# Inputs of grouped quads laid by rounds, source rows asked for six items ahead, prepared data written an item later

## The chip, the cores and the metric

The kernel runs on one core of one Trainium2 chip. Times are device microseconds of one execution; lower is better. The time before is 2416.06 us, the median of three runs (2413.56 to 2433.85).

## The reference

A graph layer with 6,250 nodes, 200,000 edges sorted by target, 128 features and 20 edge attributes:

```python
h = relu(layernorm(x))
xw = h @ W_in
W_ij = (softplus(edge_attr @ W_f1 + b_f1) - log 2) @ W_f2 + b_f2
W_ij = W_ij * edge_weight
out = segment_sum(xw[dst] * W_ij, src, 6250)
return x + (softplus(out @ W_o1 + b_o1) - log 2) @ W_o2 + b_o2
```

The target of an edge (`dst`, sorted) says which row of `xw` is read, and the source (`src`, random) says into which row the product is summed.

## The kernel before

Edges are handled in quads of 512 (four chunks of 128), 391 in all. `Plan` orders them into 414 **items**: 207 single quads ("S"), 184 grouped quads ("B") in 23 **rounds** of eight, and 23 items "V" for what overflows from a round. After the first dozen items S and B take turns, so a round spans 17 items.

The order of work is written out by hand. The main loop (line 1304) runs once per item i, and at named points of it calls hooks that were registered with `at(i, point, function, ...)`: "L" at the beginning (loads), "D0" to "D2" and "DM" (VectorE), "A0" to "A2" (ScalarE), "PE2" (TensorE), "S" at the very end. Each engine takes its instructions in that order, and SyncE (SP), which issues nearly all loads and writes, does so too: an issue that has to wait for its data holds everything behind it.

An item's own work: `s1_pe` makes the first layer's matmul, one item ahead; `s1_exp` (line 362, one instruction an item) and `s1_ln` make the softplus; `s2_pe_w` the second layer; `s2_m` (line 604) multiplies by the gathered rows. A single quad is then compared for equal sources and scattered to DRAM by POOL with indirect DMAs that add (`scatter`, line 672). The single quads 16 to 191 are "listed": in windows of 16 their comparisons are made ahead by `l_eq` (line 418), two quads at a time, at point "DM", where `s2_m` of the item stands behind it.

What the change touches:

- **Source rows.** `sb_load` (line 385) brings the 512 sources of each of two quads, spread to all partitions, 128 KB a row, into a tile `sb` with four buffers. `s1_eq` (line 403) and `l_eq` read it. For the listed quads it is asked for two items ahead of `l_eq` (line 1257), for the others two items ahead of the quad. The first window's rows are needed at items 6 to 13, interleaved with the rows of the first single quads.
- **Inputs of a round.** `nat_load` (line 681) runs three items ahead of a round's ranking. The inputs lie in DRAM in the order of the edges, and a round takes every second quad. It issues four loads: the attributes `fn` (8 runs of 336 bytes a partition), the targets `dn` (8 runs of 16 bytes) and two for the window bases `bn` (each 8 runs of 8 bytes, the same for all partitions). `nat_1` to `nat_4` split `fn` in three bf16 parts into `sts`, `nat_max` (line 698) takes its largest value, and `nat_win` turns targets and bases into one-hot columns.
- **Preparation of nodes.** 25 groups of 256 nodes (the last of 128) go through layernorm and `W_in`; for all but the first the steps are spread over items t0-3 to t0+3, one group about every nine items, the last at items 213 to 216. `prep_x3` (line 266) makes the last part, and `tab_write` (line 271), called from it at point "D2" of item t0+3, writes the group to the DRAM table `tab`, from which `load_pair` and `load_win` read windows. `base_caps` (line 1661) keeps a window's start within the groups that are written by then.
- **Features of single quads.** `fb_1` to `fb_4` split 4,096 edges at a time; `fb_4` ends with the write to `fsd` (line 297), from which `load_pair` takes `ft`. `load_pair` runs `SLEAD` = 4 items ahead of its first quad and has three buffers.

Further lines that the profile names: 188 `xt_load`, 277 `fb_load`, 313 to 321 `load_pair`, 328 `load_win`, 687 to 690 `nat_load`, 500 `l_load`, 653 `s3_ji`.

Of the kernel before, what the change touches and what calls it, by code (L numbers as in the profile page):

```python
# [7 lines left out]
F32 = mybir.dt.float32  # L8
BF16 = mybir.dt.bfloat16
I32 = mybir.dt.int32  # L10
# [4 lines left out]
AX = mybir.AxisListType  # L15
# [5 lines left out]
P = 128  # L21
# [19 lines left out]
PLEAD = 7  # L41
WLEAD = 6
SLEAD = 4
CQ = 16
EARLY_N = 256
BLK = 4
# [6 lines left out]


@with_exitstack
def tile_gnn(ctx: ExitStack, tc: tile.TileContext, x, fS, fN, cT, srcT, srcr, dstr, dstT, base0, win_, wf1, wfB, wf2,
             bias, bo1c, wo1, wo2, consts, sel, ident, cmap, out, n_edges):
    nc = tc.nc
    N = out.shape[0]
# [202 lines left out]
    def prep_x3(g):  # L262
        o, T = groups[g]
        w = T * P
        x3 = pst[g]["x3"]
        nc.vector.tensor_tensor(x3[:, :T, 2], pst[g]["rm"][:, :T], x3[:, :T, 1], op=ALU.subtract)
        tab_write(g)

    def tab_write(g):
        o, T = groups[g]  # L270
# [23 lines left out]
    def fb_4(b):  # L294
        f3 = fst[b]["f3"]
        nc.vector.tensor_tensor(f3[:, 2], fst[b]["fr"], f3[:, 1], op=ALU.subtract)
        nc.sync.dma_start(fsd[b].rearrange("g (p e) -> p g e", p=P), f3)
        del fst[b]

# [374 lines left out]

    rk = {}

    def cols(t, w, q, d, n):
        v = t[:, w * q:w * (q + d * (n - 1)) + w]
        return v if n == 1 else bass.AP(v.tensor, v.offset, [v.ap[0], [w * d, n], [1, w]])

    def nat_load(r):
        fn = wk.tile([P, RND, 4 * KN], F32, tag="fn", name="fn", bufs=1)
        dn = wk.tile([P, RND, 4], I32, tag="dn", name="dn", bufs=1)
        bn_ = wk.tile([P, 2, RND, 2], I32, tag="bn0", name="bn0", bufs=1)
        for j, dj, q, d, n in runs(pl.rounds[r]):
            v = slice(j, j + dj * (n - 1) + 1, dj)
            nc.sync.dma_start(fn[:, v] if n > 1 else fn[:, j], cols(fN, 4 * KN, q, d, n))
            nc.sync.dma_start(dn[:, v] if n > 1 else dn[:, j], cols(dstT, 4, q, d, n))
            for k in range(2):
                nc.sync.dma_start(bn_[:, k, v] if n > 1 else bn_[:, k, j],  # L690
                                  cols(base0[k:k + 1].to_broadcast([P, base0.shape[1]]), 2, q, d, n))
        rk[r] = {"fn": fn.rearrange("p j (c k) -> p (j c) k", k=KN), "dn": dn, "bn": bn_}

    def nat_1(r):
        nc.scalar.copy(sts[r % 2][:, :, 1:1 + KN], rk[r]["fn"])

    def nat_max(r):
        nc.vector.tensor_reduce(fmax[:, NB + r:NB + r + 1], rk[r]["fn"].rearrange("p x k -> p (x k)"), axis=AX.X,
                                op=ALU.max, apply_absolute_value=True)

    def nat_2(r):
# [11 lines left out]
    def nat_win(r):  # L713
        t = sts[r % 2]
        b = wk.tile([P, RND, 2], F32, tag="nb", name="nb", bufs=1)
        nc.vector.scalar_tensor_tensor(b, rk[r]["bn"][:, 0], 0.0, rk[r]["bn"][:, 1], op0=ALU.max, op1=ALU.min)
        rel = wk.tile([P, RND, 2, 2], F32, tag="nrel", name="nrel", bufs=1)
        nc.vector.tensor_tensor(rel.rearrange("p j h c -> p (j h) c"), rk[r]["dn"].rearrange("p j (h c) -> p (j h) c", c=2),
                                b.rearrange("p j h -> p (j h)").unsqueeze(2).to_broadcast([P, 2 * RND, 2]), op=ALU.subtract)
        for h in range(2):  # L720
            o = t.rearrange("p (j h c) k -> p h j c k", h=2, c=2)[:, h, :, :, KZ + h * WIN:KZ + (h + 1) * WIN]
            nc.vector.tensor_tensor(o, rel[:, :, h].unsqueeze(3).to_broadcast([P, RND, 2, WIN]),
                                    iot[:, :WIN].unsqueeze(1).unsqueeze(1).to_broadcast([P, RND, 2, WIN]), op=ALU.is_equal)
# [220 lines left out]
    with tc.manual_schedule():  # L944
# [83 lines left out]
        prep_mm(0)  # L1028
        fb_3(0)
        fb_4(0)  # L1030
        rel0 = [rel(0, k * SEG, (k + 1) * SEG) for k in range(2)]
        prep_x1(0)
        prep_rm(0)
        prep_x2(0)
        prep_x3(0)
        for k in range(2):
            src_cast(0, k * SEG, (k + 1) * SEG, nc.gpsimd)
        ws = cp.tile([K1, P], BF16, name="ws")
# [29 lines left out]
        def at(i, point, fn, *a):  # L1068
            hooks.setdefault((i, point), []).append((fn, a))
# [31 lines left out]
        for g in range(1, NG):  # L1101
            t0 = pl.prep(g)
            at(t0 - 3, "L", xt_load, g)
            at(t0 - 1, "D2", prep_stat, g)
            at(t0, "A1", prep_rs0, g)
            at(t0, "D2", prep_norm, g)
            at(t0 + 1, "PE2", prep_tp, g)
            at(t0 + 2, "A0", prep_relu, g)
            at(t0 + 2, "PE2", prep_mm, g)
            at(t0 + 3, "A0", prep_x1, g)  # L1110
            at(t0 + 3, "DM", prep_rm, g)
            at(t0 + 3, "A2", prep_x2, g)
            at(t0 + 3, "D2", prep_x3, g)
        for b in range(1, NB):
            t0 = max(2, pl.ps[b * BE // SEG] - SLEAD - 4)
            if b > 1:
                at(max(0, t0 - 3), "L", fb_load, b)
            at(t0, "A1", fb_1, b)
            at(t0, "D2", fb_2, b)
            at(t0 + 1, "A1", fb_3, b)  # L1120
            at(t0 + 1, "D2", fb_4, b)

        busy = units | {pl.prep(g) + k for g in range(1, NG) for k in range(5)}
        mid = clear(NQ // 2, busy, 2) - 6
# [126 lines left out]
        for w in range(NW):  # L1251
            for g in range(4):
                n = LB + SW * (w - 1) + 4 * g
                i = pl.ps[n] + 2 if w else 6 + 2 * g
                for k in range(2):
                    kk = (LB + SW * w + 4 * g) // 2 + k
                    at(max(0, i + k - 2), "L", sb_load, kk)
                    at(i + k, "DM", l_eq, kk)
                if w:
                    i = clear(i + 2, units)  # L1260
                    at(i, "PE2", l_count, (LB + SW * w) // 4 + g)
                else:
                    at(i + 1, "PE2", l_count, LB // 4 + g, (0,))
                    i += 2
                    at(i, "PE2", l_count, LB // 4 + g, (1,))
                at(i + 1, "D0", l_dup, w, g)
            i += 1
            at(i, "D0", l_scan, w)
            i = clear(i, units)
            at(i, "PE2", l_before, w)  # L1270
            at(i + 1, "D0", l_index, w)
            assert i + 1 <= pl.ps[LB + SW * w] + 1
            at(i + 2, "D2", l_id, w)
            i = clear(i + 3, units)
            at(i, "PE2", l_place, w)
            at(i + 1, "D0", l_take, w)
            i = clear(wend[w] + 12, units)
            at(i, "L", l_start, w)
            at(i, "A0", l_dg, w)
            at(i, "PE2", l_row, w)  # L1280
            at(i + 1, "D0", l_same, w)
            k = clear(i + 1, units)
            at(k - 1, "L", l_load, w)
            at(k, "PE2", l_sum, w)
            at(k + 1, "A0", l_copy, w)
            at(k + 1, "DM", l_ji, w)
            at(k + 1, "A2", l_int, w)
            at(k + 2, "S", l_scatter, w)
# [86 lines left out]
    with tc.For_i(0, trips, 1) as ci:  # L1375
# [15 lines left out]
        sb = wk.tile([P, P], I32, bufs=1, tag="oeq", name="fsb")  # L1391
        nc.sync.dma_start(sb, srcr.rearrange("s e -> (s e)")[bass.ds(ci * P, P)].unsqueeze(0).to_broadcast([P, P]))
        fn = wk.tile([P, KN], F32, tag="fn", name="ffn", bufs=1)
        nc.sync.dma_start(fn, fN[:, bass.ds(ci * KN, KN)])
        fr = wk.tile([P, KN], F32, tag="nr", name="ffr", bufs=1)
        fp = wk.tile([P, KZ], BF16, tag="oh", name="ffp")
        nc.vector.memset(fp[:, 0:1], 1.0)
# [237 lines left out]
    return i  # L1635


def runs(qs):
    for step in (1, 2, 3):
        if all(qs[k + 2 * step] - qs[k + step] == qs[k + step] - qs[k] for k in range(len(qs) - 2 * step)):  # L1640
            return [(j, step, qs[j], qs[j + step] - qs[j], len(qs[j::step])) for j in range(step)]
    return [(j, 1, q, 1, 1) for j, q in enumerate(qs)]


def node_groups(n):
    first = min(EARLY_N, n)
    return [(0, first // P)] + [(o, min(2, (n - o) // P)) for o in range(first, n, 256)]
# [2 lines left out]
def base_caps(n, nq):  # L1650
    pl = Plan(nq)
    groups = node_groups(n)
    at = {}
    for k, q in enumerate(pl.sq):
        at[q] = pl.ps[k // 2 * 2] - SLEAD
    for q in pl.bo:
        at[q] = pl.perm[q] - WLEAD + 4
    caps = []
    for s in range(-(-nq // 2)):
        i = min(at[q] for q in (2 * s, 2 * s + 1) if q in at)  # L1660
        ready = min([groups[g][0] for g in range(1, len(groups)) if pl.prep(g) + 3 >= i] or [n])
        caps.append(ready - WIN)
    return caps


def _layout(inputs):
# [25 lines left out]
    caps[:-(-nq // 2)] = base_caps(np_, nq)  # L1692
    sq = np.array(pl.sq + [nq - 1] * (-len(pl.sq) % (be // SEG)))
    fs = fp.reshape(-1, SEG, rb)[sq].reshape(-1, be, rb).transpose(0, 2, 1)
    fn = np.concatenate([fp, cpad[:, None]], 1).reshape(-1, P, rb + 1).transpose(1, 0, 2).reshape(P, -1)
    base0 = np.stack([dstp[::WSEG], np.repeat(caps, SC // WSEG).astype(dstp.dtype)])
    sel = np.zeros((P, 3), np.float32)
    sel[[rb + 1, 2 * rb + 2, 3 * rb + 3], 0] = 1.0
    sel[KX, 1:] = 1.0
# [17 lines left out]
    for r in range(3):  # L1717
# [8 lines left out]
        "srcT": srcp.reshape(-1, P)[cols].T,  # L1726
        "srcr": srcp.reshape(-1, SC),
        "dstr": dstp.reshape(-1, SC),
        "dstT": dstp.reshape(-1, P).T,
        "base0": base0,  # L1730
        "win": np.asarray(inputs[p + "W_in"]),
        "wf1": np.concatenate([wf1] * 6 + [bf1[None]] * 3, 0),
# [30 lines left out]
```

## Time and profile before

| | |
|---|---|
| median of three runs | 2416.06 us |
| profiled execution | 2406.39 us, span 2404.6 us |
| mean granted TensorE clock | 0.863 |
| PE busy | 1975.6 us (82%) |
| PE weight loads | 1389.7 us (58%) |
| DVE busy | 1717.5 us (71%) |
| ACT busy | 1257.1 us (52%) |
| POOL busy | 1583.2 us (66%) |
| DMA packets | 419,278, 224.64 MB, 162,227 of them under 512 B |
| SP's wait at line 271 for the DVE | 376.1 us in 23 waits |
| SP's wait at line 297 for the DVE | 194.7 us in 16 waits |

Busy times of different engines lie beside each other. "A <- B" names an engine's instruction that stood idle and what ended that wait. A row of the windows view gives a stretch of the span in us, its length, the busy time of PE, PEld, DVE, ACT and POOL with the count of instructions, then the granted clock, the mean share of DMA time and GB/s. Instructions of the SP queue (SPq) take time to issue; the transfer itself runs afterwards.

### The profile page before, as it was taken

Reading aid. Unit: us, or ns where it says so; the run is one execution under the profiler, and the core shown is the slowest. Engines: PE = TensorE matmul, PEld = TensorE weight load, DVE = VectorE, ACT = ScalarE, POOL = GpSimd, SP = SyncE. Lnnn points to the kernel's source line nnn. Section 1 sums busy time; section 2 is a strip of 40 time slices with the busy share of each in tenths; the row PEclk is TensorE's granted clock in tenths of the full one; section 3 lists DMA queues with packets and bytes.
Section 4 is the critical chain, followed back from the end, with each engine's and each line's share of the span. In section 5 each row is a group of like instructions: output and inputs, shape, how many; then the busy total and the mean of one; then the engine's idle time right before and its main releaser. Section 6 shows DMA issues by size and latency. Waiting matters only on the chain. (4 is left out here: it accounts for less than half of the span.)

```text
span 2404.6 us, 58531 instructions
## 1 busy us (share of the span) xinstructions
PE 1975.6 (82%) x21648; PEld 1389.7 (58%) x21648; DVE 1717.5 (71%) x4480; ACT 1257.1 (52%) x3311; POOL 1583.2 (66%) x988
## 2 busy tenths in 40 slices
PE   2679878698897897997867988988988898999846
PEld 1567555465665565655645556656655665666734
DVE  4557669678777778867766778777878868776635
ACT  1357455455554565554545556555655555565424
POOL 4478757566666666674655676677677767776774
PEclk9678788788898888987978889988998988999867
DMA  6676544444554545544454454455455445445748
GB/s 204 181 168 112 89 73 76 83 74 82 91 74 75 91 79 90 83 69 78 70 88 71 83 90 74 73 92 86 71 87 92 76 76 79 73 68 87 148 47 233
DMA packets 419278, 224.64 MB, mean 93 GB/s; under 512 B 162227, under 2 KB 398550, under 8 KB 418990
## 3 DMA queue, kind: packets, MB, share of 16 engines
q0 software_dynamic: 135520, 67.56, 27.8%
q1 hardware_dynamic: 283038, 153.25, 24.1%
q8 instruction: 170, 2.79, 0.5%
q14 instruction: 118, 0.97, 0.1%
q10 hardware_dynamic: 432, 0.08, 0.0%
HBM read 121.80 MB, written 98.94 MB: 92 GB/s over the span
## 5 line engine op out<-in xcount | busy, mean ns | idle before, releaser
L672 POOL DMA_INDIRECT acc<-s,lji x704 | 1166.5, 1657 | 498.7 <-DVE s L604 174.0
L362 ACT ACTIVATE a<-z 128x512 f32<-128x512 f32 x414 | 252.2, 609 | 560.5 <-PE z L336 502.7
L577 PE MATMUL W<-w,a 128*128 128x128 f32 x3312 | 544.1, 314 | 0.0
L672 POOL DMA_INDIRECT acc<-s,ji x215 | 350.0, 1628 | 258.2 <-ACT ji L653 160.0
L577 PEld LDWEIGHTS W<-w,a 128*128 128x128 f32 x3312 | 457.6, 214 | 71.9 <-issue 53.6
L882 PE MATMUL un<-so,bm 32*128 32x392 bf16 x2944 | 342.8, 359 | 12.4 <-DVE ldup L434 5.6
L882 PE MATMUL un<-so,rem 32*128 32x392 bf16 x2944 | 330.1, 357 | 0.0
L882 PE MATMUL un<-so,low 32*128 32x392 bf16 x2944 | 326.1, 352 | 0.0
L604 DVE TENSOR_TENSOR s<-W,xc 128x512 f32<-128x512 f32 x230 | 158.7, 690 | 216.5 <-ACT xc L586 180.6
L367 ACT ACTIVATE a<-a,con 128x512 f32<-128x512 f32 x414 | 298.8, 722 | 13.6
L586 ACT ACTIVATE xc<-xg,cb 128x128 f32<-128x128 f32 x828 | 239.5, 386 | 95.3 <-PE xg L565 44.2
L797 DVE TENSOR_SCALAR pm<-iot,pos 128x576 bf16<-128x576 f16 x736 | 239.3, 387 | 26.1 <-PE po L809 25.2
L893 DVE TENSOR_TENSOR accT<-un,accT 128x392 f32<-128x392 f32 x352 | 174.2, 556 | 116.8 <-PE un L882 116.5
L808 PE MATMUL pf<-pm,st 128*108 128x512 bf16 x736 | 244.2, 423 | 6.4 <-ACT s L627 3.9
L594 ACT ACTIVATE xc<-xgb,ex 128x128 f32<-128x128 f32 x736 | 207.3, 363 | 0.0
L869 DVE TENSOR_SCALAR so<-iot,ex 128x392 bf16<-128x392 f16 x736 | 193.7, 325 | 0.0
L339 PE MATMUL xgb<-wb,bfe 42*128 42x128 bf16 x2208 | 190.5, 221 | 3.5 <-DVE accT L893 3.5
L418 DVE TENSOR_TENSOR eql<-sb,srcT_sb 128x1024 bf16<-128x1024 int16 x88 | 107.0, 1216 | 110.0 <-DMA sb<-src 100.9
L809 PE MATMUL po<-pm,st 128*108 128x64 bf16 x736 | 146.0, 198 | 41.4 <-DVE ex L832 33.6
L336 PE MATMUL z<-bfe,wsb 64*128 64x512 bf16 x552 | 178.4, 392 | 0.2
L565 PE MATMUL xg<-wn,oh 63*128 63x128 bf16 x828 | 92.4, 240 | 100.9 <-DVE oh L378 84.8
L882 PEld LDWEIGHTS <-bm 32*128 32x128 bf16 x2944 | 122.8, 101 | 90.4 <-issue 56.8
(233 smaller groups left out, 3239.1 us busy)
## 6 DMA issues: line engine op xcount, KB each, us to landing
sb<-src SPq DMA_DIRECT2D x207, 128.0 KB
rb<-reld SPq DMA_DIRECT2D x207, 64.0 KB
fsd<-f SPq DMA_DIRECT2D x26, 480.0 KB
ft<-fsd SPq DMA_DIRECT2D x103, 120.0 KB
acc<-s,lji POOLq DMA_INDIRECT x704
ta_in<-acc SPq DMA_DIRECT2D x36, 256.0 KB
fb<-in_fS_dram SPq DMA_DIRECT2D x26, 320.0 KB
ft<-fsd SPq DMA_DIRECT2D x103, 80.0 KB
```

Source lines behind the costliest of these rows:

```text
L336: yield nc.tensor.matmul(z, wsb[:n, k], ft[:n], start=(k == 0), stop=(k == 2))
L339: nc.tensor.matmul(xg[:, c, :], ft[KZ:KX, c * P:(c + 1) * P], wn[KZ:KX, k, :], start=(k == 0), stop=(k == 2))
L362: nc.scalar.activation(a, st[q]["z"], AF.Exp)
L367: nc.scalar.activation(a, a, AF.Ln, bias=half, scale=0.5)
L577: nc.tensor.matmul(W[:, c, :], st[n]["a"][:, c * P:(c + 1) * P], w2, start=False, stop=(c == 3))
L586: nc.scalar.mul(xc[:, c, :], st[n]["xg"][:, c, :], v)
L594: nc.scalar.mul(xc[:, c, :], xg[:, c, :], bq[q]["ex"][:, c, 0:1])
L672: nc.gpsimd.indirect_dma_start(out=accs[k][:rows, :], out_offset=bass.IndirectOffsetOnAxis(ap=ji, axis=0), in_=s, in_offset=None, compute_ ...
L797: nc.vector.tensor_scalar(pm[:, c], iot[:, :SLOTS], rk[r]["pos"][:, 4 * j + c:4 * j + c + 1], None, op0=ALU.is_equal)
L808: nc.tensor.matmul(f[:KS], w, pm[:, c, :GRP * CAP], start=(c == 0), stop=(c == 3))
L869: nc.vector.tensor_scalar(so, iotw[:, :GN], bq[q]["ex"][:, s, 1:2], None, op0=ALU.is_equal)
L882: nc.tensor.matmul(ts[g][:, :GN], parts[k][v, j, :], sos[j][v], start=(j == 0 and k == 0), stop=(j == RND - 1 and k == 2))
```

## The change

- The host lays `fN` in the order of the rounds and puts the target beside the 20 attributes and the weight, so that a row has 22 numbers; `nat_load` takes a round's rows with one load. The input `dstT` and the helpers `cols` and `runs` go. `dn` becomes a view of the 22nd column, and `nat_max` runs over all 22.
- `base0` is laid by rounds too, both kinds of base side by side, and comes with one load of 32 numbers a partition.
- `sb` rows of listed quads are asked for six items ahead (`SBLEAD`) instead of two.
- `tab_write` is taken out of `prep_x3` and stands at point "S" of item t0+4; the write to `fsd` is taken out of `fb_4` and stands at "S" one item later (for the second block at the end of the same item). `base_caps` counts a group as ready one item later.

```diff
+SBLEAD = 6
...
         nc.vector.tensor_tensor(x3[:, :T, 2], pst[g]["rm"][:, :T], x3[:, :T, 1], op=ALU.subtract)
-        tab_write(g)
...
         nc.vector.tensor_tensor(f3[:, 2], fst[b]["fr"], f3[:, 1], op=ALU.subtract)
+
+    def fb_write(b):
+        f3 = fst[b]["f3"]
         nc.sync.dma_start(fsd[b].rearrange("g (p e) -> p g e", p=P), f3)
...
     def nat_load(r):
-        fn = wk.tile([P, RND, 4 * KN], F32, tag="fn", name="fn", bufs=1)
-        dn = wk.tile([P, RND, 4], I32, tag="dn", name="dn", bufs=1)
+        fn = wk.tile([P, 4 * RND, KN + 1], F32, tag="fn", name="fn", bufs=1)
+        o = 4 * (NS + RND * r) * (KN + 1)
+        nc.sync.dma_start(fn.rearrange("p x k -> p (x k)"), fN[:, o:o + 4 * RND * (KN + 1)])
         bn_ = wk.tile([P, 2, RND, 2], I32, tag="bn0", name="bn0", bufs=1)
-        for j, dj, q, d, n in runs(pl.rounds[r]):
-            v = slice(j, j + dj * (n - 1) + 1, dj)
-            nc.sync.dma_start(fn[:, v] if n > 1 else fn[:, j], cols(fN, 4 * KN, q, d, n))
-            nc.sync.dma_start(dn[:, v] if n > 1 else dn[:, j], cols(dstT, 4, q, d, n))
-            for k in range(2):
-                nc.sync.dma_start(bn_[:, k, v] if n > 1 else bn_[:, k, j],
-                                  cols(base0[k:k + 1].to_broadcast([P, base0.shape[1]]), 2, q, d, n))
-        rk[r] = {"fn": fn.rearrange("p j (c k) -> p (j c) k", k=KN), "dn": dn, "bn": bn_}
+        nc.sync.dma_start(bn_.rearrange("p k j h -> p (k j h)"),
+                          base0[0:1, 4 * RND * r:4 * RND * (r + 1)].to_broadcast([P, 4 * RND]))
+        rk[r] = {"fn": fn[:, :, :KN], "all": fn, "dn": fn.bitcast(I32)[:, :, KN], "bn": bn_}
...
-        nc.vector.tensor_reduce(fmax[:, NB + r:NB + r + 1], rk[r]["fn"].rearrange("p x k -> p (x k)"), axis=AX.X,
+        nc.vector.tensor_reduce(fmax[:, NB + r:NB + r + 1], rk[r]["all"].rearrange("p x k -> p (x k)"), axis=AX.X,
...
             at(t0 + 3, "D2", prep_x3, g)
+            at(t0 + 4, "S", tab_write, g)
...
             at(t0 + 1, "D2", fb_4, b)
+            at(t0 + 1 if b == 1 else t0 + 2, "S", fb_write, b)
...
-                    at(max(0, i + k - 2), "L", sb_load, kk)
+                    at(max(0, i + k - SBLEAD), "L", sb_load, kk)
...
-        ready = min([groups[g][0] for g in range(1, len(groups)) if pl.prep(g) + 3 >= i] or [n])
+        ready = min([groups[g][0] for g in range(1, len(groups)) if pl.prep(g) + 4 >= i] or [n])
...
-    fn = np.concatenate([fp, cpad[:, None]], 1).reshape(-1, P, rb + 1).transpose(1, 0, 2).reshape(P, -1)
-    base0 = np.stack([dstp[::WSEG], np.repeat(caps, SC // WSEG).astype(dstp.dtype)])
+    fn = np.concatenate([fp, cpad[:, None], dstp.astype(np.int32).view(np.float32)[:, None]], 1)
+    fn = fn.reshape(-1, P, rb + 2)[cols].transpose(1, 0, 2).reshape(P, -1)
+    base0 = np.stack([dstp[::WSEG], np.repeat(caps, SC // WSEG).astype(dstp.dtype)]).reshape(2, -1, 2)
+    base0 = np.concatenate([base0[:, qs].reshape(-1) for qs in pl.rounds])[None]
```

More of the change, by code (lines that the diff above doesn't have):

```diff
@@ L55, in tile_gnn @@
 @with_exitstack
-def tile_gnn(ctx: ExitStack, tc: tile.TileContext, x, fS, fN, cT, srcT, srcr, dstr, dstT, base0, win_, wf1, wfB, wf2,
+def tile_gnn(ctx: ExitStack, tc: tile.TileContext, x, fS, fN, cT, srcT, srcr, dstr, base0, win_, wf1, wfB, wf2,
              bias, bo1c, wo1, wo2, consts, sel, ident, cmap, out, n_edges):
@@ L675, in tile_gnn @@
     rk = {}
-    def cols(t, w, q, d, n):
-        v = t[:, w * q:w * (q + d * (n - 1)) + w]
-        return v if n == 1 else bass.AP(v.tensor, v.offset, [v.ap[0], [w * d, n], [1, w]])
     def nat_load(r):
-        fn = wk.tile([P, RND, 4 * KN], F32, tag="fn", name="fn", bufs=1)
-        dn = wk.tile([P, RND, 4], I32, tag="dn", name="dn", bufs=1)
+        fn = wk.tile([P, 4 * RND, KN + 1], F32, tag="fn", name="fn", bufs=1)
+        o = 4 * (NS + RND * r) * (KN + 1)
+        nc.sync.dma_start(fn.rearrange("p x k -> p (x k)"), fN[:, o:o + 4 * RND * (KN + 1)])
         bn_ = wk.tile([P, 2, RND, 2], I32, tag="bn0", name="bn0", bufs=1)
-        for j, dj, q, d, n in runs(pl.rounds[r]):
-            v = slice(j, j + dj * (n - 1) + 1, dj)
-            nc.sync.dma_start(fn[:, v] if n > 1 else fn[:, j], cols(fN, 4 * KN, q, d, n))
-            nc.sync.dma_start(dn[:, v] if n > 1 else dn[:, j], cols(dstT, 4, q, d, n))
-            for k in range(2):
-                nc.sync.dma_start(bn_[:, k, v] if n > 1 else bn_[:, k, j],
-                                  cols(base0[k:k + 1].to_broadcast([P, base0.shape[1]]), 2, q, d, n))
-        rk[r] = {"fn": fn.rearrange("p j (c k) -> p (j c) k", k=KN), "dn": dn, "bn": bn_}
+        nc.sync.dma_start(bn_.rearrange("p k j h -> p (k j h)"),
+                          base0[0:1, 4 * RND * r:4 * RND * (r + 1)].to_broadcast([P, 4 * RND]))
+        rk[r] = {"fn": fn[:, :, :KN], "all": fn, "dn": fn.bitcast(I32)[:, :, KN], "bn": bn_}
     def nat_1(r):
@@ L717, in nat_win @@
         rel = wk.tile([P, RND, 2, 2], F32, tag="nrel", name="nrel", bufs=1)
-        nc.vector.tensor_tensor(rel.rearrange("p j h c -> p (j h) c"), rk[r]["dn"].rearrange("p j (h c) -> p (j h) c", c=2),
+        nc.vector.tensor_tensor(rel.rearrange("p j h c -> p (j h) c"), rk[r]["dn"].rearrange("p (x c) -> p x c", c=2),
                                 b.rearrange("p j h -> p (j h)").unsqueeze(2).to_broadcast([P, 2 * RND, 2]), op=ALU.subtract)
@@ L1030, in tile_gnn @@
         fb_4(0)
+        fb_write(0)
         rel0 = [rel(0, k * SEG, (k + 1) * SEG) for k in range(2)]
@@ L1035, in tile_gnn @@
         prep_x3(0)
+        tab_write(0)
         for k in range(2):
@@ L1393, in tile_gnn @@
         fn = wk.tile([P, KN], F32, tag="fn", name="ffn", bufs=1)
-        nc.sync.dma_start(fn, fN[:, bass.ds(ci * KN, KN)])
+        nc.sync.dma_start(fn, fN[:, bass.ds(cr * (KN + 1), KN)])
         fr = wk.tile([P, KN], F32, tag="nr", name="ffr", bufs=1)
@@ L1635, in clear @@
     return i
[L1638 to L1642, printed above, removed]
 def node_groups(n):
@@ L1728, in _layout @@
         "dstr": dstp.reshape(-1, SC),
-        "dstT": dstp.reshape(-1, P).T,
         "base0": base0,
```

## The prediction, made before the result was known

> **What bounds the kernel now.** I read the page first, then windows cut by round, the waits of the engines and of the SP queue, and the SP timeline around one long wait. Line L362 runs once per item, so its 414 starts clock the items, and 17 items make a round. The first view is busy time by round (PE, PEld, DVE, ACT, POOL, then the granted clock, DMA share, GB/s).
>
> ```profile
> 641.10:729.30 88.20, 76.58 (x901) 52.72 (x900) 69.31 (x182) 49.75 (x134) 61.95 (x39) 0.92 0.50 76
> 1196.90:1300.90 104.00, 79.30 (x908) 56.74 (x907) 70.47 (x186) 50.59 (x138) 60.25 (x38) 0.85 0.45 73
> 1300.90:1399.00 98.10, 80.97 (x891) 53.95 (x892) 68.07 (x186) 48.74 (x126) 60.08 (x37) 0.81 0.47 81
> 1399.00:1484.20 85.20, 75.06 (x895) 52.68 (x895) 64.83 (x158) 48.41 (x127) 61.38 (x37) 0.92 0.52 84
> ```
>
> Rounds with the same work take 85 to 106 us. The last row is a round without node preparation, and the PE fills 75 of its 85 us; all later rounds are like it (84 to 87), and there the PE is the bound. The first row has two node groups to prepare and still takes 88.2. The middle rows have 25 and 17 us of idle PE and a lower clock, and no engine is full in them. Who is waited for between 248 and 1330 us, first by the DVE, then by the SP queue:
>
> ```profile
> DVE eql L418 <- DMA sb<-src: 83.0, 9, 13.6
> ...
> SPq L271 <- DVE x L266: 255.2, 15, 31.9
> SPq L271 <- DVE so L869: 57.9, 3, 22.0
> ```
>
> Nine times the DVE stands before a comparison because its source row has not landed, 83.0 us in all; from 1330 to 2200 us that wait does not occur. Meanwhile SP, which issues every load in one order, stands at L271 (the write of prepared rows to `tab`) until the DVE has made them. What SP does after such a stand, and the machine beside it:
>
> ```profile
> 1192.26 0.41 SPq L687 DMA_DIRECT2D fn<-in_fN_dram  x1
> 1192.72 0.57 SPq L688 DMA_DIRECT2D dn<-in_dstT_dram  x1
> 1193.34 1.94 SPq L690 DMA_DIRECT2D bn<-in_base_dram  x2
> 1195.32 9.99 SPq L388 DMA_DIRECT2D sb<-src  x4
> ...
> 1195.00:1201.00 6.00, 2.17 (x23) 1.55 (x23) 1.93 (x5) 2.35 (x6) 5.08 (x4) 0.95 0.10 2
> 1201.00:1207.00 6.00, 0.00 (x0) 0.00 (x0) 0.00 (x0) 0.00 (x0) 0.44 (x1) 0.50 0.52 83
> 1207.00:1213.00 6.00, 1.11 (x7) 0.92 (x8) 2.45 (x6) 0.00 (x0) 3.58 (x3) 0.50 0.83 216
> ```
>
> The four `sb` issues take 9.99 us; the median issue of L388 is 432 ns, so 1.73 was due. Ahead of them stand the two `bn` loads, 8 KB each, in runs of 8 bytes: 2 x 128 partitions x 8 quads = 2,048 packets. In the first window 2 GB/s for 6 us is 12 KB: the transfer engines do almost nothing but these. In the second next to nothing computes. So each long wait is made by two things together: SP comes late from L271 and issues the row two items before its use, and the row queues behind 16 KB of 8-byte pieces.
>
> **The start** has the same sign. Its waits, over the whole span:
>
> ```profile
> DVE eq L403 <- DMA sb<-src: 13.9, 4, 7.4
> POOL acc L672 <- ACT ji L653: 160.0, 27, 33.9
> ```
>
> The 7.4 ends at 73.2 us; that row was issued at 58.0, behind the first round's `bn` (59 to 64 us: 1 GB/s). The 33.9 is POOL's wait for its first scatter, at 75.5, just behind it. From there to about 211 us POOL runs scatter on scatter, so when it starts sets when the early items end.
>
> **The change, part by part.**
>
> 1. *Inputs by rounds.* Per round four loads become two: `fn` with the target in its 22nd column (128 runs of 2,816 bytes for 1,024 of 336 and 1,024 of 16) and `bn` (128 runs of 128 bytes for 2,048 of 8). SP's issues: 0.41 + 0.57 + 1.94 = 2.92 become about 0.41 + 0.97 = 1.4 (the `bn` rate kept), and the 8.26 us of held `sb` issues go: some 9.8 us of SP's time in each of 23 rounds. The DVE's maximum (L698, 846 ns for 672 elements) takes 704: 40 ns x 23 = **0.9 us** more. The other readers (L695 on ACT, L703 on the DVE) now step from row to row of 22 numbers; from nothing to double time, 0.85 x 23 = 20 us; I take nothing, since L703 reads one stepped operand already and takes 848 ns for 672 elements, and L711, which writes one, 847.
>
> 2. *Source rows six items ahead.* An item is 88.2 / 17 = 5.2 us, so four items are 20.8, more than the longest lateness, 13.6. Parts 1 and 2 each would remove most of the nine waits; together I count all: **-83.0**, bounds 0 (the rounds are otherwise bound) and the value of the rounds themselves. Those say: the three rounds that waited least give 88.2, 92.1 and 90.7 - 3.1 = 87.6, mean 89.3; the eleven rounds from 248.5 to 1300.9 take 1052.4, so 1052.4 - 11 x 89.3 = 70, and the twelfth falls from 98.1 to 85.2, 13 more: **83** again. The PE's lower clock in the waiting rounds is inside this second count.
>
> 3. *Writes an item later.* `tab_write` leaves the DVE point of item t0+3 for the end of item t0+4. It costs the same 0.4 us issue, and is moved past SP's loads of item t0+4; POOL's queue is not passed, for SP alone issues it. L271 waited 376.1 us in all (265.2 + 57.9 + 33.5 + 19.7). The wait shortens by the loads that now stand ahead of it (a pair load is nine issues and two reads of bases, 6.6 us by the trace from 1184 to 1190) but does not go: SP runs about four items ahead of the DVE, and meets the rows one item late instead of none. Queued behind it are the loads of item t0+5 on; when it ends SP is one item ahead instead of level. Pair loads have 3 items in hand, window loads 4 or more, `xt` 2: enough, if SP spends about 11.3 us on four items against the DVE's 20.8 (a pair load 6.6, two window loads 1.95 each, a row load 0.8). Nothing itself; **+3** for chance lateness, bounds 0 and 41 (below). The feature write (L297) moves likewise; `ft<-fsd` then has one item instead of two to see it land. It landed in 7.7 us (1105.2 to 1112.9), and stands on SP alone; the price without that cover is 2.5 us x 25 = 62 of SP time, which was 29.2 already. The clamp on table windows moves by the same item (`base_caps`, +4): at item 100 the targets are near 410 and 2,816 rows are prepared, so no window is cut.
>
> 4. *The early row buffers.* Against the gain of part 2 stands `sb`'s four buffers. In items 0 to 8 the listed rows (needed from item 6) are now asked for among the rows needed at once; some ten loads find no free buffer, and SP waits for a DVE comparison at each. The fourth listed row waits for item 6, and behind it stand the pair load and the row that item 7 needs: 6.6 + 0.9 of issues and some 3 to land, 11 us; before, the DVE stood 12.0 at that place (its eql at 105.1). Meanwhile POOL has a backlog at 2.1 us a scatter. I take no loss, bounds 0 and 10 x 13.6 = 136. The first round's clog gone lets the first scatter go 7.4 us earlier, and POOL's holes of 5.0 and 1.9 at 173 to 177 us, under the second round's `bn`, should shrink: **-10**, bounds -18 and, with the buffers, far above nothing.
>
> Sum: -83 + 0.9 + 3 - 10 = **-89**. The profiled execution took 2406.4 (span 2404.6), so 2317; the median of the runs stands 9.7 above it, 2416.1, so **2327**.
>
> The row at 1201 to 1213 us shows the clock at 0.50 after the PE's stand. [...]
>
> **Rivals.**
>
> *A. The lateness moves to another load.* SP still stands at L271 some 300 us, and `xt`, asked for two items ahead, or `ft` becomes the late one. For it: the wait is moved, not removed. Against: between 248 and 1330 us no engine lists a wait for `xt`, `ft`, `rb` or `wn`, with SP later than it will be. Half of the nine waits back: +41, 2368.
>
> *B. More.* The prepared rounds go to 87.6 instead of 89.3 (11 x 1.7 = 19) and the start gives 18 instead of 10: 2300. For it: PE takes 79 to 85 us in waiting rounds for instructions that take 76.6 at 0.92.
>
> *C. Hidden anyway.* The DVE's waits lie beside work that PE needs; then little comes off: the extra idle PE time of the longest round alone, 24.7 - 10.1 = 14.6, and the 7.4 at the start, 22: 2394. Against: the same excess stands in most rounds before 1399, and none after.
>
> *D. Slower, by the buffers.* SP stands behind the early comparisons in items 2 to 8. Ten loads at the longest wait, 13.6, are 136: 136 - 89 = +47, 2463. It decides from 8.9 us a load on. For it: the buffers are indeed short; against: the DVE already runs at 9 to 12 us an item there, held by POOL.
>
> That the change doesn't do what it says would show as 8-byte runs still in the packets; the new layout's run of 32 numbers leaves no room for it.
>
> **How the numbers follow.** Forecast 0.64; A 0.12; B 0.17; C 0.04; D 0.03. The range reaches from just below B to just beyond A, 2296 to 2374. The runs spread over 0.8%, so 1% (24 us) is about what can be told from no change. Faster by over 1% are the forecast, A and B: 0.93; within 1% C: 0.04; slower D: 0.03.
>
> **What would show it.** The line eql <- sb gone from the DVE's waits between 248 and 1330 us; rounds there of 87 to 91 at a clock near 0.9; L388's issues at 0.4 us after `bn`; some 88,000 fewer packets (4,096 a round become 256, in 23 rounds); L271's waits still over 200 us and harmless; first scatter near 68 us; later rounds at 84 to 87 as before. Wrong would be: rounds still near 98 with another load named, or item 13 reached after 141 us, or later rounds shorter by more than 2 us each.

## The result, and the profile after

| | before | after |
|---|---|---|
| median | 2422.51 us (2413.56 to 2433.85, 4 runs) | **2327.76 us** (2317.32 to 2336.04, 4 runs) |
| profiled execution, span | 2406.39, 2404.6 | 2336.04, 2334.2 |
| mean granted clock | 0.863 | 0.885 |
| DMA packets, under 512 B | 419,278, 162,227 | 330,221, 70,227 |
| PE busy | 1975.6 | 1963.9 |
| first scatter starts | 75.5 | 67.4 |

The changed kernel takes 0.9604 of the time of the one before, 95% interval 0.9539 to 0.967. Run again in five rounds it gives 2326.41 against 2410.45: 0.9646, interval 0.9615 to 0.9677. The prediction was 2327.0. The profiled execution of after is the longest of its four, and that of before lies below all four of its runs, so the two traces differ by 70 us and the medians by 95 and 84.

**A clock to compare by.** The starts of the softplus exponential (L362 before, L365 after) divide the span into stretches of the same work. The prediction used them too, but its numbers run two ahead: its item 13, reached at 141 us before, is item 11 here, and its rounds begin at items 33, 50 and so on instead of 35 and 52. (Two semaphore waits of ACT, at 30.0 and 32.8 us, carry the same line and would explain it.) Seventeen items are a round from either start, but what falls into one differs. Cut at 35, the late rounds alternate. Windows of after (columns as in the prediction), items 239 to 256 and 256 to 273:

```profile
1340.67:1417.47 76.80, 71.27 (x872) 50.24 (x869) 56.15 (x136) 47.88 (x126) 54.31 (x34) 0.92 0.46 75
1417.47:1511.07 93.60, 79.14 (x916) 55.11 (x913) 77.10 (x207) 48.85 (x130) 66.28 (x41) 0.92 0.50 87
```

They take about 77 and 94 us with some 34 and 41 scatters, pair after pair, and a pair takes some 170. Cut at 33, the late rounds of both kernels take 82 to 87 us each, with 36 or 37 scatters. The table compares stretches of several rounds, for which either cut will do. With the cut at 35 the traces divide so (us; the rest is all that follows item 392, the end of the program included):

| kernel | to item 13 | 13-35 | 35-239 | 239-392 | rest |
|---|---|---|---|---|---|
| before | 155.8 | 107.3 | 1150.4 | 751.9 | 239.2 |
| after | 145.0 | 100.8 | 1094.9 | 755.4 | 238.2 |
| after, second profile | 144.0 | 100.7 | 1088.2 | 748.1 | 237.8 |

Items 35 to 239 are the rounds that prepare nodes. They lose 55 to 62 us, items 13 to 35 another 7, the start 11 to 12; the late rounds scatter by 4 in either direction.

**The waits.** Before, the DVE stood nine times for a listed source row, 83.0 us. The waits of after in the same stretch (235 to 1260 us; us in total, times, longest), first the DVE's two largest, then the SP queue's at L271:

```profile
DVE s L607 <- ACT xc L589: 77.4, 51, 4.7
DVE accT L888 <- PE un L877: 44.8, 25, 4.0
...
SPq L271 <- DVE x L267: 158.7, 11, 21.3
...
SPq L271 <- DVE pm L792: 70.3, 5, 17.7
SPq L271 <- DVE so L864: 54.6, 3, 20.2
SPq L271 <- DVE lsel L480: 34.6, 2, 18.6
```

No wait of the DVE for `sb` is left there, while SP stands at L271 (still the write to `tab`) for 318 us: in this kernel a queue that stands long is no loss by itself. What SP does around a round's inputs in after, and the windows beside it:

```profile
1126.58 0.37 SPq L683 DMA_DIRECT2D fn<-in_fN_dram  x1
1127.00 0.42 SPq L685 DMA_DIRECT2D bn<-in_base_dram  x1
1138.67 0.40 SPq L271 DMA_DIRECT2D tab<-x  x1
```

```profile
1126.50:1129.50 3.00, 3.00 (x26) 1.89 (x25) 1.63 (x4) 2.24 (x6) 2.62 (x2) 1.00 0.80 161
1129.50:1138.00 8.50, 8.02 (x85) 5.74 (x84) 3.11 (x10) 5.85 (x19) 6.06 (x5) 1.00 0.41 40
```

The bases take one issue of 0.42 us, and the transfer engines move 161 GB/s in the three microseconds around it, where before they moved 2 for six. SP then stands 11 us at L271, and PE is busy for 8.0 of the next 8.5 us.

**What stays.** The busy time of the whole prepared stretch, before and then after:

```profile
263.06:1413.48 1150.42, 964.70 (x10834) 660.59 (x10834) 862.46 (x2336) 607.69 (x1625) 731.06 (x445) 0.86 0.48 79
```

```profile
245.74:1340.67 1094.93, 960.11 (x10833) 656.52 (x10831) 862.78 (x2342) 605.02 (x1625) 730.64 (x446) 0.89 0.49 84
```

Of the 55.5 us that came off, PE's idle time gave 50.9 (185.7 became 134.8) and its busy time only 4.6. At each of the nine places PE still stands idle for about 4 us in after, now for the DVE's own work and not for a row. At these places and in the two items behind them, the idle stretches of PE over 2.5 us add up to 105.9 us before and 40.5 after. The waits of PE in the prepared rounds of after:

```profile
PE xg L568 <- DVE oh L381: 37.0, 19, 4.1
PE po L804 <- DVE ex L827: 21.7, 8, 5.3
PE rkp L742 <- DVE ex L827: 12.5, 3, 4.7
```

A short stand cost the clock here no less than a long one. The 8 us behind a stand of 14.7 us (before, to 1211.9; clock 0.65) and the 8 us behind one of 4.9 (after, to 896.8; clock 0.50):

```profile
1211.90:1219.90 8.00, 8.00 (x48) 6.30 (x49) 3.86 (x10) 3.87 (x10) 4.53 (x4) 0.65 0.55 98
```

```profile
896.80:904.80 8.00, 7.51 (x57) 4.78 (x60) 6.85 (x21) 6.09 (x16) 3.88 (x3) 0.50 0.53 111
```

Twelve such stands of 3.7 to 5.3 us in the prepared rounds of after are each followed by 8 us at 0.50 to 0.52; behind the five stands of 11 to 15 us of before it was 0.50 to 0.74 (part of the half clock falls within the long stand: the one of 14.7 us has 0.61 from its start to its end). It is not always so. At the three places where the row came only 2.6 to 3.6 us late, before had two stands each, of 4.0 to 5.0 us, and the 8 us behind these six lay anywhere between 0.50 and 0.82. At item 153 both kernels have a stand, of 4.5 and 4.9 us: in after it is the one above, and before, with another stand just ahead of it, it was followed by

```profile
934.70:942.70 8.00, 7.52 (x105) 4.84 (x108) 7.52 (x22) 6.24 (x16) 2.82 (x3) 0.82 0.47 102
```

PE is busy for 7.5 us of the 8 in both, with 57 matmuls in after and 105 before: where the first of the two stands went, the clock behind the second was 0.50 instead of 0.82 and took back what was won.

Whether the length of a stand decides on the clock behind it, the runs do not show. Behind a stand of 3.7 us (after, to 804.7) the 8 us were at 0.50, behind one of 3.1 (before, to 1020.7) at 0.50 as well, and behind one of 4.5 (before, to 934.7) at 0.82. The clock brought little: PE's busy time in the prepared rounds fell by 4.6 us, and by 8.7 in the second profile. That fits stands which became shorter and did not go.

### The profile page after: what moved, and what is told of

Read it like the earlier page. It is cut to its first block, busy times and chain, and to the rows that moved or that the text cites. A ratio compares the mean times of both kernels' runs of the same rounds, so it can differ in the third digit from the quotient of the medians.

```text
span 2334.2 us, 58464 instructions
## 1 busy us (share of the span) xinstructions
PE 1963.9 (84%) x21648; PEld 1384.1 (59%) x21648; DVE 1712.8 (73%) x4480; ACT 1253.4 (54%) x3311; POOL 1574.1 (67%) x988
## 2 busy tenths in 40 slices
DMA packets 330221, 224.63 MB, mean 96 GB/s; under 512 B 70227, under 2 KB 306550, under 8 KB 329934
## 5 line engine op out<-in xcount | busy, mean ns | idle before, releaser
L675 POOL DMA_INDIRECT acc<-s,ji x215 | 352.7, 1640 | 327.1 <-ACT ji L656 244.3
L365 ACT ACTIVATE a<-z 128x512 f32<-128x512 f32 x414 | 252.1, 609 | 552.2 <-PE z L339 359.6
L568 PE MATMUL xg<-wn,oh 63*128 63x128 bf16 x828 | 92.1, 239 | 113.8 <-DVE oh L381 87.8
L804 PE MATMUL po<-pm,st 128*108 128x64 bf16 x736 | 145.0, 197 | 32.7 <-DVE ex L827 24.5
L563 PE MATMUL W<-b2rep,onesb 64*128 64x512 bf16 x414 | 168.6, 407 | 0.4 <-POOL b2rep L1051 0.4
```

The costliest lines, as they stand in the source:

```text
L365: nc.scalar.activation(a, st[q]["z"], AF.Exp)
L675: nc.gpsimd.indirect_dma_start(out=accs[k][:rows, :], out_offset=bass.IndirectOffsetOnAxis(ap=ji, axis=0), in_=s, in_offset=None, compute_ ...
```

## The experiments

All ratios are of medians against the kernel before on the same chip. Stretches of their profiles, as above:

| kernel | to item 13 | 13-35 | 35-239 | 239-392 | rest |
|---|---|---|---|---|---|
| layout_only | 147.3 | 99.3 | 1091.5 | 751.5 | 240.5 |
| bases_only | 146.4 | 103.2 | 1088.6 | 751.9 | 239.5 |
| lead_only | 157.0 | 103.8 | 1087.7 | 752.0 | 238.9 |
| writes_only | 156.6 | 107.9 | 1083.5 | 765.1 | 244.3 |
| no_layout | 154.6 | 99.4 | 1096.5 | 748.5 | 237.9 |
| no_lead | 142.9 | 99.6 | 1091.4 | 751.5 | 239.4 |
| no_writes | 143.2 | 100.2 | 1091.3 | 751.5 | 238.6 |
| first_window_2 | 144.8 | 100.1 | 1085.5 | 755.2 | 242.2 |
| bases_spread | 144.0 | 95.3 | 1094.1 | 751.8 | 239.9 |
| inputs_only | 153.9 | 112.9 | 1147.6 | 800.0 | 237.0 |
| inputs_spread | 145.2 | 99.7 | 1091.4 | 751.5 | 243.6 |

**Each part alone, on the kernel before.** The theory on record before these four, "two causes together": a row waits only when SP comes late from L271 and the bases' 8-byte reads stand ahead of it. The rivals: SP's stands alone, the early asking alone, or the 8-byte pieces alone make the waits.

layout_only is the first part of the change alone; `SBLEAD` and the writes stay as before:

```diff
+        nc.sync.dma_start(fn.rearrange("p x k -> p (x k)"), fN[:, o:o + 4 * RND * (KN + 1)])
...
+        nc.sync.dma_start(bn_.rearrange("p k j h -> p (k j h)"),
+                          base0[0:1, 4 * RND * r:4 * RND * (r + 1)].to_broadcast([P, 4 * RND]))
...
```

> Only the inputs by rounds; source rows two items ahead and writes where they were. Theory 'two causes together' (a row waits only when SP comes late from the table write AND the 8-byte pieces stand ahead of it): most of the nine DVE waits go, 15 of 83 us stay where SP is late by itself, the start is 15 us earlier: 75 to 90 us off, 2335 to 2345. Rival 'SP's stands' (the waits come from SP standing at L271, the pieces only add): half of the 83 stays, 2375. Rival 'lead': only the earlier asking counts, 2400.

2325.1 us, ratio 0.965 (0.9615 to 0.9685).

lead_only:

```diff
+SBLEAD = 6
...
-                    at(max(0, i + k - 2), "L", sb_load, kk)
+                    at(max(0, i + k - SBLEAD), "L", sb_load, kk)
```

> Only the source rows six items ahead; 8-byte pieces and writes as before. 'Two causes together': the rows now stand ahead of the pieces in SP's order, so all nine waits go, but the pieces delay some other load and the start is not earlier or is later for want of buffers: 45 to 65 us off, 2360 to 2375. 'SP's stands': the lead covers the stands too, the same 2360. 'Pieces alone' (they hold the machine whatever stands behind them): under 20 us off, over 2400.

2359.24 us, ratio 0.9799 (0.9764 to 0.9833).

writes_only:

```diff
-        tab_write(g)
...
+            at(t0 + 4, "S", tab_write, g)
...
+            at(t0 + 1 if b == 1 else t0 + 2, "S", fb_write, b)
...
-        ... if pl.prep(g) + 3 >= i] or [n])
+        ... if pl.prep(g) + 4 >= i] or [n])
```

> Only the table and feature writes an item later. 'SP's stands': each stand frees the loads of one more item, the rows come some 5 us earlier at each of nine waits, 30 to 45 us off, 2375 to 2390. 'Two causes together': SP is one item ahead instead of level but the rows still queue behind the pieces, 10 to 30 us off, 2390 to 2412. 'Pieces alone': nothing, 2415 to 2425.

2355.89 us, ratio 0.9746 (0.9681 to 0.981).

bases_only leaves `fn` and `dn` as before and lays only the bases by rounds:

```diff
-            for k in range(2):
-                nc.sync.dma_start(bn_[:, k, v] ..., cols(base0[k:k + 1].to_broadcast([P, base0.shape[1]]), 2, q, d, n))
+        nc.sync.dma_start(bn_.rearrange("p k j h -> p (k j h)"),
+                          base0[0:1, 4 * RND * r:4 * RND * (r + 1)].to_broadcast([P, 4 * RND]))
...
```

> Only the window bases by rounds (one load of 128-byte runs for two of 8-byte runs); attributes and targets as before in 336- and 16-byte runs. 'Two causes together' with the 8-byte runs as the second: all but 5 us of what the layout gives alone, 2335 to 2350. If the 16- and 336-byte runs count as much per packet as the 8-byte ones: half of it, 2375 to 2385.

2332.41 us, ratio 0.9687 (0.9653 to 0.9722).

In the profiles of all four the prepared rounds fall from 1150 us to between 1084 and 1092, as far as in after. The DVE's wait for listed rows there, 83.0 before, is 3.5 in layout_only, 5.9 in bases_only, 2.4 in writes_only and not listed in lead_only. So any one of three parts ends the nine waits, and the parts don't add. That is more than the theory said: it gave the later writes 10 to 30 us and "SP's stands" gave them 30 to 45, and they brought 50. The theory was widened after these runs (any one of three things taken away is enough), and the kernels below put it to the test.

What the profiles show to set the four apart is the start: 146 to 147 us to item 13 with the bases by rounds, 157 without, and the first scatter at 66.9 and 67.8 against 74.0 and 75.5. The layout of the bases alone is nearly the whole change. Two things stay open. The profile of lead_only is the fastest of its five runs (2341.18 us, the median 18 more), so it does not show where the median run spends the rest; and the 13 us that the late rounds of writes_only took more were not traced to a cause.

**One part taken back, on the kernel after.** no_lead asks for all rows two items ahead, no_writes has both writes where they were, and first_window_2 asks for the first listed window's rows two items ahead and for all others six:

```diff
no_lead
-                    at(max(0, i + k - SBLEAD), "L", sb_load, kk)
+                    at(max(0, i + k - 2), "L", sb_load, kk)
no_writes
+        tab_write(g)
...
-            at(t0 + 4, "S", tab_write, g)
...
-            at(t0 + 1 if b == 1 else t0 + 2, "S", fb_write, b)
first_window_2
-                    at(max(0, i + k - SBLEAD), "L", sb_load, kk)
+                    at(max(0, i + k - (SBLEAD if w else 2)), "L", sb_load, kk)
```

after_again is the changed kernel itself, beside them.

> The changed kernel itself, for comparison on one chip with the three that follow. After the first four runs the theory is: the long wait needed three things at once (SP late from the table write, the row asked for two items ahead, 8-byte pieces ahead of it), so that taking away any one ends it; only the pieces also cost at the start. By that 0.960 to 0.968 of the kernel before. By 'the parts add up' (0.965, 0.980 and 0.975 multiplied): 0.922.

> The changed kernel with source rows two items ahead again. 'Any one is enough': within 0.3% of the changed kernel; up to 8 us faster, if the want of row buffers in items 2 to 8 costs something. If the lead carries a share of the gain: 20 us or more slower than it.

> The changed kernel with the table and feature writes back in their place. 'Any one is enough': within 0.3% of the changed kernel. If the later writes carry a share: 20 us or more slower.

> The changed kernel, but the rows of the first listed window (eight loads, needed at items 6 to 13) are asked for two items ahead again; all later ones six. If the want of row buffers in items 2 to 8 costs time (the DVE's waits of 13.2 and 7.8 us at 100 and 118 us): these two waits go and 5 to 12 us come off. If POOL's scatters set the pace there anyway: within 3 us of the changed kernel.

| | median | ratio | interval |
|---|---|---|---|
| after_again | 2326.41 | 0.9646 | 0.9615 to 0.9677 |
| no_lead | 2325.8 | 0.9649 | 0.9623 to 0.9676 |
| no_writes | 2326.47 | 0.9653 | 0.9623 to 0.9683 |
| first_window_2 | 2329.61 | 0.9664 | 0.9638 to 0.9691 |

None can be told from after. With the layout, six items of lead and the later writes are worth nothing that these runs can tell, and layout_only, which has neither, agrees. The shortage of `sb` buffers is there: in the first 240 us of after,

```profile
DVE eq L406 <- DMA sb<-src: 24.9, 3, 13.2
```

where first_window_2 waits 8.1 and, at its `eql`, 7.3 us for `sb` in the whole span; but it takes no less time, so this wait lies beside what sets the start.

**no_layout** is the kernel before with the other two parts together:

```diff
+                    at(max(0, i + k - SBLEAD), "L", sb_load, kk)
...
+            at(t0 + 4, "S", tab_write, g)
...
+            at(t0 + 1 if b == 1 else t0 + 2, "S", fb_write, b)
...
```

> Source rows six items ahead and writes an item later, inputs as before with their 8-byte runs. 'Any one is enough': the prepared rounds are as short as in the changed kernel and nothing comes off at the start, so the time is that of the lead or the writes alone: 48 to 58 us off, ratio 0.975 to 0.980. If the two still add up: 0.955.

2339.45 us, ratio 0.9736 (0.9681 to 0.9791): 67 us off where 48 to 58 were expected, with an interval of 50 to 77. Again the prepared rounds are as short as in after (1096.5) and the start is not (154.6).

**What makes the bases' reads slow.** They are 2,048 packets of 8 bytes, and all 128 partitions read the same few addresses. bases_spread keeps packets, sizes and issues as before and gives each partition a copy of its own in DRAM:

```diff
-                                  cols(base0[k:k + 1].to_broadcast([P, base0.shape[1]]), 2, q, d, n))
+                                  cols(base0[:, k * NSC * 4:(k + 1) * NSC * 4], 2, q, d, n))
...
+    base0 = np.repeat(base0.reshape(1, -1), P, 0)
```

> The kernel before, with the bases copied once per partition in DRAM, so that each partition reads its own 8-byte runs instead of all 128 the same ones; the number and size of the packets are the same. If the shortness of the runs makes them slow: 10 to 14 us for the 2,048 packets of a round as before and the time of the kernel before. If the one address read by all makes them slow: 2 to 4 us a round, as the 16-byte targets take, and a ratio of 0.97, that of the bases by rounds alone.

2335.78 us, ratio 0.9716 (0.9671 to 0.9761), with the same 419,278 packets as before. SP at the place that the prediction showed, and the window from there:

```profile
1136.87 0.57 SPq L688 DMA_DIRECT2D dn<-in_dstT_dram  x1
1137.49 1.99 SPq L690 DMA_DIRECT2D bn<-in_base_dram  x2
1139.52 2.00 SPq L388 DMA_DIRECT2D sb<-src  x4
```

```profile
1139.00:1141.00 2.00, 2.00 (x23) 1.48 (x22) 1.86 (x4) 0.18 (x1) 1.70 (x2) 1.00 0.99 40
```

The four `sb` issues take 2.00 us instead of 9.99. From the first to the last of a round's 2,048 packets it takes 1.5 to 2.9 us (median 2.0 of 23 rounds), and 10.2 to 14.6 before (median 12.2). So neither the length of the runs nor their number made the 12 us by itself, but that they all read one place in DRAM. (The targets, 1,024 reads of 16 bytes a round from places of their own, take 0.6 to 1.8 us in before, less than that expectation says.) After still reads one place, but with 128 runs of 128 bytes, in 0.6 to 2.0 us. What in the place makes 2,048 reads of it slow was not tried. The DVE still waits six times for listed rows in the prepared rounds of bases_spread, 15.4 us in all, and these rounds are as short as in after all the same.

**The inputs without the bases.** inputs_only lays `fn` and the targets by rounds, in one load, and leaves the bases as before:

```diff
+        nc.sync.dma_start(fn.rearrange("p x k -> p (x k)"), fN[:, o:o + 4 * RND * (KN + 1)])
...
+                b = base0[k:k + 1].to_broadcast([P, base0.shape[1]])[:, 2 * q:2 * (q + d * (n - 1)) + 2]
+                nc.sync.dma_start(bn_[:, k, j:j + dj * (n - 1) + 1:dj],
+                                  bass.AP(b.tensor, b.offset, [b.ap[0], [2 * d, n], [1, 2]]))
```

> Attributes and targets of a round with one load (2,816-byte runs), bases still in 8-byte runs; row lead and writes as before. If the 8-byte runs are the whole of the layout's gain: SP saves one issue a round and the pieces stay, under 20 us off, ratio over 0.99. If the count of packets is what matters, half of them are gone: ratio 0.975 to 0.985.

2449.78 us, ratio 1.0161 (1.0096 to 1.0226): half of the layout makes the kernel 1.6% slower, which neither expectation had. The DVE's nine waits stay,

```profile
DVE eql L418 <- DMA sb<-src: 81.6, 9, 13.5
```

and the late rounds, which had no such wait before, take 48 us more. PE and windows at one of the places, where PE stands for nothing that the profile shows:

```profile
1726.65 1.05 PE L577 MATMUL W<-w,a 128*128 128x128 f32 x7
1731.63 0.37 PE L577 MATMUL W<-w,a 128*128 128x128 f32 x1 [3.94 <-issue]
```

```profile
1727.70:1731.60 3.90, 0.00 (x0) 0.00 (x0) 0.25 (x2) 0.44 (x2) 0.00 (x0) 0.82 0.68 154
1731.60:1740.00 8.40, 8.37 (x60) 5.29 (x60) 1.46 (x3) 4.18 (x12) 7.13 (x5) 0.50 0.37 40
```

The bases' packets run here from 1718.0 to 1730.3; a 16 KB packet of the instruction queue starts at 1729.2 and takes 1.0; PE goes on at 1731.6. Four such stands (2.0, 3.9, 3.8 and 2.6 us, at items 266, 300, 317 and 351) lie in just the four late rounds that grew most, by 6.6, 9.3, 13.7 and 11.3 us: 40.9 of the 48. The lower clock behind the stands (0.50 in the second window, and in the 8.4 us behind the stand of 3.8) makes up most of what the stands themselves do not: PE is busy for 706.9 us of the late rounds at a mean clock of 0.87, and for 673.2 at 0.92 before. The kernel before has none of these stands; in seven of its last eight rounds a packet of that queue is under way just as the bases' reads begin, within 0.4 us of the first. The reading from this is that a load of PE's code is held up by the bases; against it stands that before has such packets in the midst of the reads too (at 1464.0 and 1802.0) and PE does not stand. The test keeps inputs_only whole and copies the bases per partition, as bases_spread does:

```diff
-                b = base0[k:k + 1].to_broadcast([P, base0.shape[1]])[:, 2 * q:2 * (q + d * (n - 1)) + 2]
+                b = base0[:, k * NSC * 4 + 2 * q:k * NSC * 4 + 2 * (q + d * (n - 1)) + 2]
...
+    base0 = np.repeat(base0.reshape(1, -1), P, 0)
```

> The inputs alone laid by rounds (fn with the target, one load), which had been slower than the kernel before (2449.8 us), now with the bases copied once per partition in DRAM; the 2,048 reads of 8 bytes and SP's order of issues stay as they were. Theory (the bases' reads of one address hold up a code load of the PE, which then stands 2 to 4 us at L577 at four places of the later rounds and runs at half clock behind it): the 8-byte reads end in 1.5 to 3 us, no stand of the PE at L577 put down to issue, items 239 to 392 take 750 to 757 us instead of 800, and the whole lies at 0.96 to 0.975 of before, 2318 to 2345. Rival (the new layout of the inputs itself costs the later rounds their 48 us, by the stepped reads of ACT and the DVE or by the packets of 2,816 bytes): items 239 to 392 stay near 800 and the whole ends at about 2375, 0.985 to 0.99 of before.

2330.68 us, ratio 0.9663 (0.9626 to 0.97). Items 239 to 392 take 751.5 again, PE has no stand put down to issue at L577, and the 8-byte reads take 1.2 to 3.1 us. So the slow reads of one place made the loss, and the new layout of the inputs costs nothing. That it is PE's code that waits behind them is only read from the places and times of the packets; it was not tried by itself.

## Why the prediction was right, and where its steps were not

- **The cause of the nine waits** was right: SP late, a row asked late, and the bases' reads ahead of it. The trace has the wait gone, L271's waits still 318 us in the prepared rounds and harmless (foreseen: over 200), and 89,057 fewer packets (foreseen: 88,000).
- **"Runs of 8 bytes"** was the wrong property. It is not the shortness by itself, but 2,048 reads of one shared place: 12.2 us a round (median) in before, 2.0 from separate copies (bases_spread). The forecast for this change is the same: its layout keeps the place and makes 128 reads of the 2,048. For an edit that only gives each partition a copy it would have been wrong.
- **The term of the waits, -83, was mis-sized.** Over the prediction's own twelve rounds (items 33 to 237), which hold all nine waits, 64 us came off in the first profile and 71 in the second. Two steps failed. First, the DVE's wait was put down one to one to the time. The six waits of 8.3 to 13.6 us, 73.6 together, gave 61.6 and 65.6 us in their rounds, but the three of 2.6 to 3.6, 9.4 together, gave only 3.3 and 3.5. In two of these three rounds (from items 135 and 152) a stand of PE of some 4 us went, but PE's busy time rose by 3.0 and 3.4 us behind the stand that stayed, and nothing came off. Second, the check by rounds ("83 again") took 89.3 us for a round that doesn't wait, from two rounds without a wait (92.1 and 88.2) and one with, less its wait (87.6). The third round without a wait was left out:

```profile
1006.60:1097.10 90.50, 81.10 (x908) 55.51 (x907) 69.62 (x179) 50.94 (x136) 61.46 (x38) 0.87 0.48 74
```

With 92.1, 88.2 and 90.5 the mean is 90.3, and the check gives 59.5 + 13 = 72. The first eleven rounds of after take 91.1 us on average and 90.3 in the second profile, the twelfth 84.4 and 86.5 (foreseen 85.2). So the two counts agreed at 83 by the choice of the three rounds.

- **"The PE's lower clock in the waiting rounds is inside this second count"**: PE's busy time in these rounds fell by 4.6 and 8.7 us only. Rival B, which asked for more of this, fell with it; its 18 at the start did not come either.
- **The start, -10:** to item 13 it was -10.8 and -11.8, with the first scatter at 67.4 (foreseen near 68). Some 2 us of it are lost again by item 33. It comes with the bases alone: lead_only and writes_only do not have it.
- **The parts.** "Parts 1 and 2 each would remove most of the nine waits" was right, and part 3 does so too, which was not seen. Writes later (+3) and the row buffers (0, up to 136): nothing to measure by no_writes and first_window_2. `nat_max`, +0.9, lies below what can be told: 846 ns became 879, 0.8 us in 23 rounds. The stepped reads that were taken at nothing cost nothing: the DVE's takes 848 ns in before and in after, ACT's 797 in both (median).
- **The total** of 2327 is met by the median of 2327.76, and not by the sum of its steps: for the -89 foreseen the first pair of traces gives -70 and the second profile -86, and the medians lie 95 and 84 apart. That it came within 1 us is luck, inside the spread of the runs.
- **The signs of "wrong"**: by the prediction's own count item 13 (item 11 here) was reached at 125.9 us, late rounds differ by 3.5 us over nine, and the DVE waits for no other load. Of the hoped-for 87 to 91 us a round, the first eleven prepared rounds, cut as there, take 88.9 to 94.0, and 87.7 to 95.6 in the second profile.

## What to carry to other kernels

The small table that every partition reads cost here by where it lay: 2,048 reads of 8 bytes took 10.2 to 14.6 us a round from one place and 1.5 to 2.9 from separate copies, and 128 reads of 128 bytes from one place 0.6 to 2.0. Where a table is read like this, try a copy for each partition, or one longer run, before tuning the order of loads around it. When a wait has several necessary causes, each fix alone ends it and the gains do not add: undo one at a time before keeping three. Before a wait is counted one to one, look what stands at the same place in rounds without it, and take all of these rounds for the yardstick, not some.

## What the runs showed of the hardware

- 2,048 reads of 8 bytes by 128 partitions took 10.2 to 14.6 us from one place in DRAM (before), and from separate copies 1.5 to 2.9 (bases_spread) and 1.2 to 3.1 us (inputs_spread). Other transfers waited meanwhile: SP's next four issues took 9.99 us at one place of before and 2.00 at the same place of bases_spread, and POOL waited 163 us in the whole span for its own scatters in before, 37 with the copies (bases_spread). That loads of code waited too, with PE standing 2 to 4 us, is read from the trace of inputs_only and not tested.
- Stands of PE of 3.7 to 5.3 us were followed by 8 us at a clock of 0.50 to 0.52 at twelve places of after; behind one of 14.7 us (before) it was 0.65. The stands that became shorter saved their length, and little of the clock: in the prepared rounds PE's idle time fell by 50.9 us and its busy time by 4.6.
